# Inverse square roots on VectorE: a bit-pattern guess and three Newton steps instead of Sqrt and reciprocal, in a two-layer convolution kernel

## The chip, the cores and the metric

The kernel runs on one core of a Trainium2 chip. The metric is device time in microseconds (us) of that core, from launch to the last write. The core has five engines with their own instruction queues: TensorE (PE, matrix products into PSUM), VectorE (DVE), ScalarE (ACT), GpSimd (POOL) and SyncE (SP, which issues most DMAs). Each engine works its queue in order; an instruction waits for semaphores that other engines or DMAs set.

## The reference

The input x has shape (8, 256, 64, 64) in fp32. Two layers follow, each a residual: `x = x + L0(gn(x))` and then `x = x + L1(gn(x))`. The normalisation is a group norm over 32 groups of 8 channels, without weights:

```python
g = v.reshape(B_, G, C_ // G, H_, W_)
m = jnp.mean(g, axis=(2, 3, 4), keepdims=True)
s = jnp.var(g, axis=(2, 3, 4), keepdims=True)
return ((g - m) / jnp.sqrt(s + eps)).reshape(v.shape)
```

Layer 0 makes 3x3 kernels from the data: two 1x1 maps to 32 channels, one of them unfolded 3x3, then batch norm (with given mean and variance, so another `1 / sqrt(v + eps)`), relu, a 1x1 map, batch norm, relu, and a 1x1 map to 9 weights for each of 32 groups at each pixel. These weigh the 3x3 neighbourhood of a third 1x1 map of 256 channels.

Layer 1 is the sum of two branches, each times a rate: 7x7 local attention with 4 heads of 64 channels and reflecting edges, and two depthwise 3x3 convolutions summed with a softmax over 9 weights (a 256 to 2304 map, `Wfc`).

Inverse roots are needed for 8 images x 2 layers of group norm, and once each for the two batch norms.

## The kernel before, in words

**Tiling.** An image is cut into 8 bands of 8 rows (512 pixels); 256 channels are two tiles of 128 partitions. The main loop runs over g, the bands of all images in sequence (64 bands of layer 1). For each g there are 8 steps s (channel tile ct = s // 4, group of pixel tiles m = s % 4). Layer 0 runs 12 bands ahead of layer 1 (`AHEAD`), so g starts at -12: the first 12 bands are layer 0 alone, the following 52 do layer 1 of one band and layer 0 of a later band side by side, and the last 12 are layer 1 alone.

**Order.** Inside the main loop the order of instructions on every engine is written out by hand (`tc.manual_schedule()`). Each step has six places; `advance()` moves to the next place and emits what is due there, and `after(n, f)` puts f off by n places. Each step emits on TensorE, among others: the attention scores (`scores`, L736, even m), the weighted values (`weighted_values`, L785), transposes of the probabilities (`transposed`, L773, copied by ScalarE at L775), and two rounds of `branch_weights` (four matmuls pf at L872, then Exp on ScalarE at L877). Beside them lie parts of layer 0: `value_maps` (L369), `values` (pv, L594, copied by ScalarE at L601), `tap_weights` (pw at L464, whose two products are `prod` on VectorE at L477 and are added by GpSimd at L485), and `hidden_maps` (L418, L428, L440). VectorE further has the masked scores and their extremes (`masked`, L750), the reciprocal of the exponentials' sums (`probabilities`, L765, before ScalarE's scaling at L767), the depthwise taps (L829, L855), the output adds (L804) and the reciprocal at L893.

**Buffers.** pf, pv, pw, the projections pq and pk, the transposes ptp, the value maps p, and the small results of the normalisation (pg, pb, pgc) share one PSUM tag, "gen", with 4 buffers: the matmul that takes the fifth waits until the first has been read. The products `prod` have 2 buffers.

**The normalisation.** `gn_affine` gets the statistics of a norm and emits a chain over places: at +3 a matmul averages the means over the group (a1, L237); at +5 VectorE takes them and forms the differences (a2, L246 to L250); at +10 a second matmul (a3); at +12 VectorE adds eps (a4, L258); at +14 ScalarE takes the Sqrt in place (a5, L262); at +18 VectorE takes the reciprocal and the bias (a6, L266 and L269), and `done(sc, bi)` runs in the same place.

For layer 0 (`scaled_weights`, tiles named a, called at s = 2 of every eighth band), `done` is `scale`: ScalarE multiplies w12 and w3 by sc (L296, L297, four instructions); five places later 16 matmuls bring the bias through the weights (`through`, L304), and two places after that VectorE adds the biases (`biases`, L312 to L314). w12s and w3s have one buffer; the bands that read the old ones have been issued in the steps before. In terms of the main loop this is band 3 of an image's eight (for the next but one image, from image 2 on); image 0's norm comes before the loop and image 1's in the first 12 bands.

For layer 1 (`norm_rows`, tiles named b, called in band 6 of each image for the next one), `done` is `keep`: VectorE copies sc and bi side by side (L535, L536); three places later two products spread them over channels (`by_channel`, pgc, L542), and two places after that VectorE takes them (L547). ScalarE applies them in `normalise` (L566) from the second step of band 7 on.

The batch norms use `rstd_` (L143) at the start, before the hand-written order begins.

**Activation tables.** ScalarE's activations come from a table that has to be in place. The profile shows its loads as ACT_TABLE_LOAD, under the line of the activation that they precede. The kernel uses Sqrt, Exp, Relu, Identity and Copy.

Of the kernel before, what the change touches and what calls it, by code (L numbers as in the profile page):

```python
# [9 lines left out]

F32 = mybir.dt.float32
BF16 = mybir.dt.bfloat16
AF = mybir.ActivationFunctionType
ALU = mybir.AluOpType
AX = mybir.AxisListType
# [3 lines left out]
P = 128  # L19
# [7 lines left out]
GN_EPS = 1e-5  # L27
BN_EPS = 1e-5
# [27 lines left out]
CHUNK = R * KW  # L56
NPROB = 2 * CHUNK
NEG = -1.0e30


AHEAD = NB + 4
# [25 lines left out]
def conv_layers_kernel(ctx: ExitStack, tc: tile.TileContext, ins: dict, out: bass.AP):  # L87
    nc = tc.nc
# [3 lines left out]
    const = ctx.enter_context(tc.tile_pool(name="const", bufs=1))  # L92
# [14 lines left out]
    def load(name, shape, src=None, now=True):  # L107
        t = const.tile(shape, F32, name=f"c_{name}")
        late.append(lambda: nc.scalar.dma_start(out=t, in_=ins[name] if src is None else src))
        if now:  # L110
            late.pop()()
        return t

    gmat = load("gmat", [P, P])
    par = load("par", [P, NPAR])
# [24 lines left out]
    for t in probs + x3n + h2n:  # L140
        nc.gpsimd.memset(t, 0.0)

    def rstd_(out_, var, eps):  # L143
        nc.vector.tensor_scalar(out_, var, eps, None, ALU.add)
        nc.scalar.activation(out_, out_, AF.Sqrt)
        nc.vector.reciprocal(out_, out_)


    bn1s = const.tile([P, 3], F32, name="bn1s")
    bn1b = const.tile([P, 3], F32, name="bn1b")  # L150
    bn2s = const.tile([P, 1], F32, name="bn2s")
    bn2b = const.tile([P, 1], F32, name="bn2b")
    for s, t, g, b_, m, v, n, p in (
        (bn1s, bn1b, PG, PB, PM, PV, 3, P),
        (bn2s, bn2b, PG2, PB2, PM2, PV2, 1, P),
    ):
        rstd_(s, par[:p, v : v + n], BN_EPS)
        nc.vector.tensor_mul(s, s, par[:p, g : g + n])
        nc.vector.tensor_mul(t, s, par[:p, m : m + n])
        nc.vector.tensor_sub(t, par[:p, b_ : b_ + n], t)  # L160
# [19 lines left out]
    stat = ctx.enter_context(tc.tile_pool(name="stat", bufs=2))  # L180
# [34 lines left out]
    def after(n, f):  # L215
        later.append((place[0] + n, f))
# [8 lines left out]
    def gn_affine(sts, means, name, done):  # L225


        n = len(sts)
        mv = stat.tile([P, n, 2], F32, name=f"mv_{name}", tag=f"mv{n}")
        for ct, st in enumerate(sts):  # L230
            nc.vector.bn_aggr(mv[:, ct, :], st)
        mean, var = mv[:, :, 0], mv[:, :, 1]
        gm, d, sc, bi = (stat.tile([P, n], F32, name=f"{v}_{name}", tag=f"{v}{n}") for v in ("gm", "d", "sc", "bi"))

        def group_means(v, k):
            pg = ps.tile([P, n], F32, name=f"pg_{name}_{k}", tag="gen", bufs=4)
            nc.tensor.matmul(pg, means, v, start=True, stop=True)  # L237
            return pg


        def a1():
            pg = group_means(mean, 0)
            after(2, lambda: a2(pg))

        def a2(pg):
            nc.vector.tensor_copy(gm, pg)  # L246
            for ct in range(n):
                c = slice(ct, ct + 1)
                nc.vector.tensor_scalar(d[:, c], pg[:, c], mean[:, c], None, ALU.subtract)
                nc.vector.tensor_scalar(d[:, c], d[:, c], d[:, c], var[:, c], ALU.mult, ALU.add)  # L250
            after(5, a3)

        def a3():
            pg = group_means(d, 1)
            after(2, lambda: a4(pg))

        def a4(pg):
            nc.vector.tensor_scalar(sc, pg, GN_EPS, None, ALU.add)  # L258
            after(2, a5)

        def a5():
            nc.scalar.activation(sc, sc, AF.Sqrt)  # L262
            after(4, a6)

        def a6():
            nc.vector.reciprocal(sc, sc)  # L266
            for ct in range(n):
                c = slice(ct, ct + 1)
                nc.vector.tensor_scalar(bi[:, c], gm[:, c], sc[:, c], -1.0, ALU.mult, ALU.mult)  # L269
            done(sc, bi)  # L270

        after(3, a1)
# [15 lines left out]
    def scaled_weights(b):  # L288
# [21 lines left out]
        def biases(pb):  # L310
            im.bias = w0.tile([P, 1 + NCT], F32, tag="bias", name=f"bias_{b}")
            nc.vector.tensor_add(im.bias[:, 0:1], pb[:, 0:1], par[:, PB21 : PB21 + 1])  # L312
            for ct in range(NCT):
                nc.vector.tensor_add(  # L314
                    im.bias[:, 1 + ct : 2 + ct], pb[:, 1 + ct : 2 + ct], chan[:, ct, CB3 : CB3 + 1]
                )

        gn_affine([im.st0[:, ct] for ct in range(NCT)], gmat, f"a{b}", scale)

    def small_maps(b, i, home):  # L320
# [208 lines left out]
    def norm_rows(b):  # L529
        im = images[b]  # L530


        def keep(sc, bi):
            both = stat.tile([P, 2], F32, name=f"both_{b}", tag="both")
            nc.vector.tensor_copy(both[:, 0:1], sc)  # L535
            nc.vector.tensor_copy(both[:, 1:2], bi)  # L536
            after(3, lambda: by_channel(both))

        def by_channel(both):
            pg = ps.tile([P, NCT, 2], F32, tag="gen", name=f"pgc_{b}", bufs=4)  # L540
            for ct in range(NCT):
                nc.tensor.matmul(pg[:, ct], gc[:, ct], both, start=True, stop=True)  # L542
            after(2, lambda: take(pg))

        def take(pg):
            im.aff = stat.tile([P, NCT, 2], F32, name=f"aff_{b}", tag="aff")
            nc.vector.tensor_copy(im.aff, pg)  # L547

        gn_affine([im.st1], gq, f"b{b}", keep)
# [460 lines left out]
    with tc.manual_schedule():  # L1010

        for i, use in enumerate(("xc", "xc", "xr", "xr", "xs", None, None, None)):
            t = None
            if use is None:
                t = w1.tile([P, NCT, RP, W], F32, tag="yp", name=f"x_{i}", bufs=3)
                t = t.rearrange("p t r c -> p t (r c)")[:, :, :BAND]
# [15 lines left out]
        for g in range(-AHEAD, B * NB):  # L1032
            b, i = divmod(g, NB)
# [75 lines left out]
def _layout(inputs):  # L1109
# [59 lines left out]
    inside = (dr >= 0) & (dr < KA) & (dc >= 0) & (dc < KA)  # L1169
    arr["mask"] = np.tile(np.where(inside, 0.0, NEG).astype(f), (2, 1))  # L1170
    return {n: np.ascontiguousarray(v) for n, v in arr.items()}
# [19 lines left out]
```

## Time and profile before

| | |
|---|---|
| median of 3 runs | 3910.43 us (3908.52 to 3914.09) |
| the profiled execution | 3911.49 us, of which the trace's span is 3909.7 us |
| mean granted TensorE clock | 0.994 |
| busy: PE, DVE, ACT, POOL | 97%, 87%, 73%, 81% of the span |
| table loads | 28, of 1.283 us each |
| Sqrt activations | 18: two for batch norms, eight for each layer's group norms |
| L258 (add eps), L266 (reciprocal) | 16 each, 0.15 to 0.16 us |

"Busy" is the time in which an engine had an instruction in work. A group of the profile names the line, the engine, the operation, the tiles (result <- operands) and the count; then the busy time in us, the mean of one in ns, and the idle time just before it with what ended it. In the timeline the first column is the start from the beginning of the span, the second the length in us; "x2" merges neighbours of one line.

### The profile page before, as it was taken

How to read it: one execution, taken by the hardware profiler on the slowest of the kernel's cores; microseconds unless marked ns; L12 is line 12 of the kernel's file. 1: busy time of each engine (PE TensorE's matmuls, PEld its weight loads, DVE VectorE, ACT ScalarE, POOL GpSimd, SP SyncE). 2: the span in 40 equal slices, each digit the busy share in tenths (PEclk: the TensorE clock that was granted, in tenths of full speed). 3: DMA queues.
4: the chain of work that ended last, by engine and by line, in shares of the span. 5: the costliest groups of instructions: out<-in, count | busy, mean ns of one | idle time of the engine just before them, and what ended most of it. 6: DMA issues, size and time to landing. Idle time of an engine off the chain costs nothing.

```text
span 3909.7 us, 71679 instructions
## 1 busy us (share of the span) xinstructions
PE 3778.1 (97%) x24620; PEld 2112.2 (54%) x24620; DVE 3419.7 (87%) x7143; ACT 2835.8 (73%) x6779; POOL 3172.5 (81%) x2156
## 2 busy tenths in 40 slices
PE   5889999999999999999999999999999999999998
PEld 2445555555555555555555555555555555555554
DVE  6879898899898999899998998989988889978778
ACT  4457777777777777777777777777777777677776
POOL 4768888888887988888888888978988888956665
PEclk9999999999999999999999999999999999999999
DMA  8764443543444543543444443444433443322221
GB/s 245 208 168 128 127 118 115 143 121 116 124 123 123 142 118 105 140 131 114 139 111 128 136 119 113 127 138 116 130 111 100 133 122 94 87 85 79 72 60 35
DMA packets 429710, 473.36 MB, mean 121 GB/s; under 512 B 60992, under 2 KB 322208, under 8 KB 429088
## 3 DMA queue, kind: packets, MB, share of 16 engines
q1 hardware_dynamic: 412768, 453.01, 41.1%
q10 hardware_dynamic: 16576, 15.76, 1.3%
q8 instruction: 194, 3.18, 0.3%
q14 instruction: 172, 1.41, 0.1%
HBM read 329.08 MB, written 143.00 MB: 121 GB/s over the span
## 4 chain that ended last, share of the span: by engine, by line
PE 41%; DVE 24%; POOL 15%; ACT 11%; issue 6%; DMA 3%; SPq 0%; ACTq 0%; POOLq 0%; DVEq 0%
PE pf L872 19%; POOL xg L485 8%; DVE prod L477 7%; DVE acc L855 5%; DVE rec L893 5%; POOL ex L1087 4%; PE small L785 3%; PE pv L594 3%; ACT x L343 3%; PE ptp L773 3%; PE sco L736 3%; PE pk L692 2%; PE pq L670 2%; ACT ex L877 2%; DMA x<-x3n 2%
## 5 line engine op out<-in xcount | busy, mean ns | idle before, releaser
L872 PE MATMUL pf<-yp,c_wfc 128*128 128x512 f32 x4096 | 1916.6, 594 | 17.8 <-ACT ex L877 6.8
L485 POOL TENSOR_TENSOR xg<-xg,prod 128x1024 f32<-128x1024 f32 x549 | 1198.8, 2184 | 106.7 <-DVE prod L477 82.5
L872 PEld LDWEIGHTS pf<-yp,c_wfc 128*128 128x128 f32 x4096 | 738.5, 190 | 719.0 <-issue 629.2
L1087 POOL TENSOR_TENSOR ex<-ex,ex 128x1024 f32<-128x1024 f32 x384 | 908.2, 2365 | 66.4 <-ACT ex L877 62.5
L829 DVE SCALAR_TENSOR_TENSOR acc<-yp,c_chan,acc 128x504 f32<-128x504 f32 (+3 forms) x1104 | 775.4, 702 | 64.7 <-ACT acc L820 41.3
L477 DVE SCALAR_TENSOR_TENSOR prod<-pw,c_par,x3q 128x1040 f32<-128x1040 f32 x576 | 737.0, 1286 | 103.6 <-PE pw L464 57.4
L855 DVE SCALAR_TENSOR_TENSOR acc<-hid,c_chan,acc 128x504 f32<-128x504 f32 (+3 forms) x1024 | 750.6, 733 | 18.1
L877 ACT ACTIVATE ex<-pf 128x512 f32<-128x512 f32 x1024 | 602.0, 588 | 214.5 <-PE pf L872 197.5
L758 ACT ACTIVATE prob<-prob,nmax 128x196 f32<-128x196 f32 x1024 | 459.1, 451 | 224.5 <-DVE nmax L750 224.3
L767 ACT ACTIVATE prob<-prob,tot 128x196 f32<-128x196 f32 x1024 | 413.1, 452 | 249.5 <-DVE tot L765 248.3
L894 POOL TENSOR_TENSOR tot<-tot,rec 128x256 f32<-128x256 f32 x254 | 185.4, 730 | 398.0 <-DVE rec L893 391.6
L893 DVE RECIPROCAL rec<-tot 128x256 f32<-128x256 f32 x256 | 445.8, 1742 | 9.5 <-POOL tot L894 4.3
L775 ACT COPY pt<-ptp 112x512 f32<-112x512 f32 x511 | 295.0, 577 | 110.3 <-PE ptp L773 109.9
L750 DVE CUSTOM_DVE_ANT_0 prob<-sco,c_mask 128x196 f32<-128x196 f32 x1024 | 324.4, 354 | 28.1 <-PE sco L736 28.0
L773 PEld LDWEIGHTS ptp<-ident,prob 128*112 128x112 f32 x2044 | 227.2, 133 | 184.2 <-issue 157.1
L773 PE MATMUL ptp<-ident,prob 128*112 128x128 f32 x2044 | 319.0, 279 | 0.0
L785 PEld LDWEIGHTS small<-pt,vt 112*64 112x64 f32 x8144 | 258.2, 137 | 77.4 <-issue 75.7
L785 PE MATMUL small<-pt,vt 112*64 112x64 f32 x8144 | 293.7, 225 | 1.2 <-DMA vt<-vd 1.2
L369 PE MATMUL p<-xc,w3s 128*128 128x512 f32 x512 | 248.3, 608 | 15.8 <-ACT ex L877 15.8
L594 PE MATMUL pv<-c_wv,yp 128*128 128x256 f32 x1056 | 252.1, 381 | 7.4 <-ACT qb L674 6.0
L888 POOL TENSOR_SCALAR tot<-tot 128x512 f32<-128x512 f32 x127 | 243.6, 1918 | 11.1
L464 PEld LDWEIGHTS pw<-h2n,c_c 128*128 128x128 f32 x1152 | 176.2, 192 | 137.6 <-issue 122.7
(139 smaller groups left out, 4750.0 us busy)
## 6 DMA issues: line engine op xcount, KB each, us to landing
vt<-vd SPq DMA_DIRECT2D x512, 112.0 KB
x3q<-x SPq DMA_DIRECT2D x128, 264.0 KB
xc<-in_x SPq DMA_DIRECT2D x64, 512.0 KB
xg<-in_xg SPq DMA_DIRECT2D x64, 512.0 KB
yp<-x SPq DMA_DIRECT2D x128, 256.0 KB
xr<-x SPq DMA_DIRECT2D x64, 512.0 KB
out_x<-xr SPq DMA_DIRECT2D x64, 512.0 KB
xs<-in_x SPq DMA_DIRECT2D x57, 512.0 KB
```

The costliest lines, as they stand in the source:

```text
L477: nc.vector.scalar_tensor_tensor(prod[:, :, :RUN], pw[:, j, :RUN].unsqueeze(1).to_broadcast([P, SHARE, RUN]), par[:, PCB2 + k : PCB2 + k + 1],
L485: nc.gpsimd.tensor_add(im.xg[i], im.xg[i], rows(prod))
L758: nc.scalar.activation(prob[:, h, :NKEY], prob[:, h, :NKEY], AF.Exp, bias=nmax[:, h : h + 1], scale=-1.0, accum_out=tot[:, h : h + 1],)
L767: nc.scalar.activation(prob[:, h, :NKEY], prob[:, h, :NKEY], AF.Copy, scale=tot[:, h : h + 1])
L773: nc.tensor.transpose(ptp[:, h, ch], prob[:, h, ch * CHUNK : (ch + 1) * CHUNK], ident)
L785: nc.tensor.matmul(po[half[h], :, t * TQ : (t + 1) * TQ], im.vt[i + ch, m][:n, t, (2 * ct + h) * HD : (2 * ct + h + 1) * HD], pt[:n, h, ch ...
L829: nc.vector.scalar_tensor_tensor(o, yp[:, ct, ra + dr : rb + dr, ca + dc : cb + dc], chan[:, ct, CW1 + k : CW1 + k + 1], o, ALU.mult, ALU.add,
L855: nc.vector.scalar_tensor_tensor(o, hid[:, ra + dr : rb + dr, ca + dc : cb + dc], chan[:, ct, CW2 + k : CW2 + k + 1], o, ALU.mult, ALU.add,)
L872: nc.tensor.matmul(pf, wfc[:, kt, 2 * m + j, ct * P : (ct + 1) * P], images[b].yp[i][:, kt, PAD : PAD + R], start=(kt == 0), stop=(kt == N ...
L877: nc.scalar.activation(ex[:, j].rearrange("p (r c) -> p r c", r=R), pf, AF.Exp)
L893: nc.vector.reciprocal(rec, v)
L1087: after(4, lambda ex=ex, exb=exb: nc.gpsimd.tensor_add(ex, ex, exb))
```

## The change

The function `rstd_` no longer uses ScalarE. It adds eps on VectorE into a second tile v, reads the bits of v as an integer, shifts them right by one, takes them from the constant 0x5F3759DF (multiply by -1 and add), and reads the result as fp32: a guess of `1 / sqrt(v)`. Three Newton steps follow, each of three VectorE instructions (t = -0.5 y y; t = t v; y = (t + 1.5) y). That is 12 VectorE instructions, each using the result of the one before it.

In `gn_affine` the steps a5 and a6 are gone: a4 calls `rstd_` and then does in the same place what a6 did, the bias and `done`. So what follows (the scalings, the matmuls L304 and L542, the biases, the copies) comes six places, one step of s, earlier in the order. One small tile, va, is added to a norm's; the differences d are reused as t.

```diff
-BF16 = mybir.dt.bfloat16
+I32 = mybir.dt.int32
...
+ROOT = float(0x5F3759DF)
...
-    def rstd_(out_, var, eps):
-        nc.vector.tensor_scalar(out_, var, eps, None, ALU.add)
-        nc.scalar.activation(out_, out_, AF.Sqrt)
-        nc.vector.reciprocal(out_, out_)
+    def rstd_(out_, var, eps, v, t):
+
+        bits = out_.bitcast(I32)
+        nc.vector.tensor_scalar(v, var, eps, None, ALU.add)
+        nc.vector.tensor_scalar(bits, v.bitcast(I32), 1, None, ALU.logical_shift_right)
+        nc.vector.tensor_scalar(bits, bits, -1.0, ROOT, ALU.mult, ALU.add)
+        for _ in range(3):
+            nc.vector.scalar_tensor_tensor(t, out_, -0.5, out_, ALU.mult, ALU.mult)
+            nc.vector.tensor_mul(t, t, v)
+            nc.vector.scalar_tensor_tensor(out_, t, 1.5, out_, ALU.add, ALU.mult)
+
+    root = [const.tile([P, 3], F32, name=f"root_{i}") for i in range(2)]
...
-        rstd_(s, par[:p, v : v + n], BN_EPS)
+        rstd_(s, par[:p, v : v + n], BN_EPS, root[0][:p, :n], root[1][:p, :n])
...
-        gm, d, sc, bi = (stat.tile([P, n], F32, name=f"{v}_{name}", tag=f"{v}{n}") for v in ("gm", "d", "sc", "bi"))
+        gm, d, sc, bi, va = (stat.tile([P, n], F32, name=f"{v}_{name}", tag=f"{v}{n}") for v in ("gm", "d", "sc", "bi", "va"))
...
         def a4(pg):
-            nc.vector.tensor_scalar(sc, pg, GN_EPS, None, ALU.add)
-            after(2, a5)
-
-        def a5():
-            nc.scalar.activation(sc, sc, AF.Sqrt)
-            after(4, a6)
-
-        def a6():
-            nc.vector.reciprocal(sc, sc)
+            rstd_(sc, pg, GN_EPS, va, d)
             for ct in range(n):
                 c = slice(ct, ct + 1)
                 nc.vector.tensor_scalar(bi[:, c], gm[:, c], sc[:, c], -1.0, ALU.mult, ALU.mult)
             done(sc, bi)
```

## The prediction

> **What bounds the kernel now.** First the page: the busy row, the chain that ended last, the costliest group.
>
> ```profile
> PE 3778.1 (97%) x24620; PEld 2112.2 (54%) x24620; DVE 3419.7 (87%) x7143; ACT 2835.8 (73%) x6779; POOL 3172.5 (81%) x2156
> ...
> PE 41%; DVE 24%; POOL 15%; ACT 11%; issue 6%; DMA 3%; SPq 0%; ACTq 0%; POOLq 0%; DVEq 0%
> ...
> L872 PE MATMUL pf<-yp,c_wfc 128*128 128x512 f32 x4096 | 1916.6, 594 | 17.8 <-ACT ex L877 6.8
> ```
>
> TensorE is the busiest, then VectorE; ScalarE, which the change relieves, has 27% free. Four pf matmuls follow each other in some 1.72 us all through the trace, so in steady state whatever delays TensorE is lost. Second, the stretches table, cut at the first pf matmul of each of six bands of one image (band 2, 3, 5 and 6 shown; first column the stretch, then its length and the busy time of TensorE, its weight loads, VectorE, ScalarE, GpSimd).
>
> ```profile
> 831.70:889.20 57.50, 57.15 (x380) 31.96 (x380) 52.29 (x107) 43.21 (x104) 50.47 (x35) 1.00 0.44 127
> 889.20:949.60 60.40, 59.37 (x401) 33.65 (x400) 54.40 (x121) 47.13 (x111) 52.98 (x37) 1.00 0.45 127
> 1007.20:1065.00 57.80, 57.20 (x380) 32.01 (x380) 52.56 (x108) 43.10 (x106) 51.17 (x36) 1.00 0.43 121
> 1065.00:1122.80 57.80, 56.18 (x380) 31.52 (x379) 53.02 (x116) 43.45 (x106) 50.63 (x35) 1.00 0.39 107
> ```
>
> Band 3 holds the layer-0 root ("a"), band 6 the layer-1 root ("b"). Band 6, table switches and all, is as long as band 5. Band 3 is 2.9 us longer, of which 1.39 us are its own 16 bias matmuls (L304). So the switches cost far less than they last.
>
> Third, the groups of ScalarE, for what is removed.
>
> ```profile
> L262 ACT ACT_TABLE_LOAD x13 | 16.7, 1283 | 0.2
> L877 ACT ACT_TABLE_LOAD x13 | 16.7, 1283 | 0.2
> L145 ACT ACT_TABLE_LOAD x1 | 1.3, 1283 | 6.8 <-DMA c_chan<-in_chan 6.8
> L758 ACT ACT_TABLE_LOAD x1 | 1.3, 1283 | 0.0
> ```
>
> Fourth, the order of time around one "a" root, VectorE (columns: start, length, engine, line, operation).
>
> ```profile
> 910.02 0.21 DVE L249 TENSOR_SCALAR d_a<-pg_a,mv_a 128x1 f32<-128x1 f32 x1
> 910.26 0.27 DVE L250 TENSOR_SCALAR d_a<-d_a,mv_a 128x1 f32<-128x1 f32 x1
> ...
> 917.90 0.15 DVE L258 TENSOR_SCALAR sc_a<-pg_a 128x2 f32<-128x2 f32 x1
> 917.97 1.29 DVE L477 SCALAR_TENSOR_TENSOR prod<-pw,c_par,x3q 128x1040 f32<-128x1040 f32 x1
> ...
> 920.25 1.29 DVE L477 SCALAR_TENSOR_TENSOR prod<-pw,c_par,x3q 128x1040 f32<-128x1040 f32 x1
> ...
> 924.47 0.16 DVE L266 RECIPROCAL sc_a<-sc_a 128x2 f32<-128x2 f32 x1
> 924.66 0.33 DVE L269 TENSOR_SCALAR bi_a<-gm_a,sc_a 128x1 f32<-128x1 f32 x2
> ```
>
> A small instruction that needs the one before it starts 0.20 us later (L266 to L269; 0.24 us from L249 to L250); one that does not, 0.07 us later (L258 to L477). VectorE has no gap here. TensorE beside it, and a "b" root's one gap (last line):
>
> ```profile
> 916.06 0.61 PE L464 MATMUL pw<-h2n,c_c 128*128 128x132 f32 x4
> ...
> 921.40 1.89 PE L594 MATMUL pv<-c_wv,yp 128*128 128x256 f32 x8
> 923.13 1.88 PE L872 MATMUL pf<-yp,c_wfc 128*128 128x512 f32 x4
> ...
> 1104.06 1.98 PE L872 MATMUL pf<-yp,c_wfc 128*128 128x512 f32 x4 [0.76 <-ACT ex L877]
> ```
>
> **Removed: ScalarE's part.** 28 loads of 1.283 us and 18 roots of 0.20 us, 39.5 us of ScalarE. After the load at L758 no other comes until the next Sqrt, through Copy, Identity, Relu and Exp, so without Sqrt one load is left, and it sits before the start's first activation. On TensorE's path the 26 loads in steady state are worth at most the gap: 0.76 us at each of 7 "b" roots (5.3 us), about nothing at the "a" roots, where TensorE runs through. The load at L758 (238.5 us) stands in the chain, so -1.28 us; bounds 0 and -1.28. The load that is left runs either in the 6.8 us that the queue idles at the start or just before L296, where w12s is not needed until the 2.51 us of L304 are over: 0, at worst +1.28.
>
> **Added: VectorE's part.** L258 and L266 give way to 12 instructions, each needing the last: 12 x 0.20 = 2.4 us. Bounds: 12 x 0.07 = 0.84 (as if none waited) and 12 x 0.24 = 2.9; I take 0.20, since the row is of the same size, engine and dependence. Three or two more (the bi pair 0.27; for "b" bi and the two copies 0.40) move up from after the reciprocal. So the product that started at 917.97 starts at 917.90 + 2.4 + 0.27 = 920.57, 2.6 us late ("b": 2.7).
>
> Queued behind on VectorE: two products (L477), the row minima (L750, ScalarE's exponentials wait), two output adds, four taps, the reciprocal of the sums (L765, ScalarE's probabilities wait). The tag "gen" has four PSUM buffers, so the pf at 923.13 takes the buffer of the pw at 916.06, read last by the product at 920.25, which ends at 921.54. Slack: 923.13 - 921.54 = 1.59 us ("b": 1098.48 - 1096.90 = 1.58). **"a", 6 times in steady state:** 2.6 - 1.6 = +1.0 us each. ScalarE's four weight scalings move up with the root: it waits for sc at 919.5 until 920.3, then they delay the transposed copy at 919.89 to 921.6, whose buffer is asked for at 924.85: nothing. The 16 bias matmuls come one step sooner, the same 1.39 us. The old values of w12s and w3s were last read in steps 0 and 1, so no wait is added. **"b", 7 times:** pgc's matmuls come a step sooner and take that buffer, so TensorE waits 1.1 us; then L765 ends at 1101.1 instead of 1098.4, L767 and L601 follow, and the next pf starts at 1102.4 instead of 1100.64; the gap of 0.76 goes and pgc's 0.44 has been paid already, so the pf of 1104.06 starts near 1104.6: +0.5 each. The last image's has no products around it: 0. Sum 6 x 1.0 + 6 x 0.5 = +9; bounds 0.07 us a step: no wait, -5.3; 0.24 us a step: 6 x 1.5 + 7 x 1.0 = +16. GpSimd's sums of products (L485) start about 1.2 us late and regain it in its gaps. No step that moves issues a DMA; SP and GpSimd's queue are not passed by one.
>
> **Start.** Image 0: L258 at 24.31 to L269 at 24.94 was 0.63 us, becomes 2.4, with all engines waiting: +1.75 (0.2 to 2.3). Image 1: the scalings go in front of the hidden map at 146.44 on ScalarE (they had followed it): +1.3 (0 to 2.5). Image 0's "b" at 201: 0 (to +1). The two batch norms: 24 small instructions for 4 on VectorE, which idles 1.18 + 0.87 + 1.08 us before 13.31: +0.3 (0 to 1.4). With -1.28: +2.1 (-1.1 to +7).
>
> **Sum:** 9 + 2 = +11 us. The profiled execution took 3911.49 us (span 3909.7 and 1.8 around it), 1.06 above the median of the runs; on the median 3910.4 + 11 = 3921.5 us.
>
> **A rule against a row.** The row: a dependent small step every 0.20 us, 2.4 us in all. The Trainium skill's "VectorE: DVE Perf Modes" (the TRN2 errata) counts 58 cycles plus the elements at 0.96 GHz, an estimate of 0.06 us for two elements, 0.75 us for twelve: below the slack, so no loss. The same page says to minimise the number of chained operations, which speaks against this change. On the loads, "ScalarE: Activation LUTs" (What ACT_TABLE_LOAD costs) adds a drain of 1.38 us to each; here the activation starts 0.01 us after the load ends (load 922.56 + 1.28, Sqrt 923.86). With the page's drain the 26 loads would last 69 us, by the rows 33.
>
> **Rivals.** *The steps overlap.* If they follow in less than about (1.59 + 0.07 - 0.27)/12 = 0.12 us, the delay stays inside the slack and the removed gaps are all that shows: -5.3 and the start's -1 to +2, about 3906. For: L258 to L477 in 0.07. Against: L249 to L250, L266 to L269. *ScalarE decides.* If the switch pairs held up the kernel, 13 x 2.57 = 33 us go: 3877. For: ex at L877 waits behind a load 13 times. Against: band 6 is no longer than band 5. *No slack at all.* If a later wait (minima, sums, GpSimd) passes on the whole insertion, 13 x 2.7 = +35, with the start's 2: 3947. For: VectorE has no gap from 909 to 924 us. Against: TensorE's next demand is 1.6 us off. *The loads stay.* With Sqrt gone nothing needs a second table; then +16 and 3926.
>
> **How the numbers follow.** Forecast 0.58, overlap 0.20, ScalarE 0.04, no slack 0.16, loads stay 0.02. A measurement here tells 0.2%, 7.8 us. The forecast's own range, 3913 to 3933, lies over +7.8 for 0.45 and under for 0.13. Overlap: 0.17 same, 0.03 faster. So faster 0.07, same 0.30, slower 0.63. The range 3907 to 3936 takes in most of the overlap and the low half of no slack.
>
> **What would show it.** One table load; 12 small VectorE steps about 0.20 us apart; band 3 near 61.4, band 6 near 58.3 us, the others unchanged; a wait of about 1 us of pf or pgc on prod L477; the first L304 at 27 us. Steps 0.1 us apart, or a pf that still starts 1.72 us after pv, would make it wrong; so would a start that hides or doubles its 2 us.

## The result, and the profile after

| | before | after |
|---|---|---|
| median, us | 3911.4 (3908.52 to 3914.09) | 3965.73 (3964.15 to 3966.02) |
| the profiled execution, us | 3911.49 | 3965.67 (span 3963.9) |
| mean granted TensorE clock | 0.994 | 0.988 |
| table loads | 28 | 1 |

The ratio of after to before is 1.0139 [1.0123, 1.0155]: 54 us slower, where +11 was forecast and 3936 was the upper end. The page of the changed kernel: the busy row, the chain's shares by engine, and two groups.

```profile
PE 3802.5 (96%) x24620; PEld 2121.2 (54%) x24620; DVE 3477.8 (88%) x7323; ACT 2810.9 (71%) x6734; POOL 3176.4 (80%) x2156
...
PE 41%; DVE 28%; POOL 11%; ACT 10%; issue 5%; DMA 3%; SPq 0%; ACTq 0%; POOLq 0%; DVEq 0%
...
L871 PE MATMUL pf<-yp,c_wfc 128*128 128x512 f32 x4096 | 1928.9, 597 | 41.5 <-ACT ex L876 20.7
...
L295 ACT ACT_TABLE_LOAD x1 | 1.3, 1283 | 8.3 <-DMA c_w<-in_w 8.3
```

VectorE did 180 more instructions and was busy 58 us longer. That is 0.32 us for each one added, where an unhindered one here lasts 0.16. The pf matmuls' idle time went from 17.8 to 41.5 us. Their busy time also grew, by 12.3 us, although there are as many as before: some of them ran slower.

The stretches table says where. These are bands 3, 5 and 6 of the same image as before (length, then the busy time of TensorE, its weight loads, VectorE, ScalarE, GpSimd, then the granted clock).

```profile
905.30:970.00 64.70, 61.59 (x401) 34.51 (x399) 58.32 (x131) 45.23 (x108) 53.55 (x37) 0.97 0.44 121
1027.60:1085.50 57.90, 57.26 (x381) 32.04 (x380) 52.62 (x110) 43.26 (x105) 51.26 (x36) 1.00 0.43 121
1085.50:1147.10 61.60, 57.91 (x380) 32.27 (x379) 56.94 (x125) 41.09 (x103) 51.14 (x36) 0.97 0.37 101
```

Band 3 (the "a" root) is 64.7 us where it was 60.4, band 6 (the "b" root) 61.6 where it was 57.8, and band 5, with no root, is as long as before. Over all images, each "a" root costs 2.8 us (four times) or 4.3 (twice), each "b" root 3.7 to 4.3, the last "b" 0.8. Bands without a root stay within 0.1 us, save the first of all (0.9). That makes some 45 us. The start, up to the first pf, took 244.9 us where it took 236.9: the other 8.

VectorE's timeline of that "a" root (start, length) shows what the roots lost.

```profile
934.02 0.15 DVE L147 TENSOR_SCALAR va_a<-pg_a 128x2 f32<-128x2 f32 x1
934.21 0.36 DVE L148 TENSOR_SCALAR sc_a<-va_a 128x2 int32<-128x2 int32 x1
934.60 2.29 DVE L149 TENSOR_SCALAR sc_a<-sc_a 128x2 int32<-128x2 int32 x1
936.92 0.16 DVE L151 SCALAR_TENSOR_TENSOR d_a<-sc_a 128x2 f32<-128x2 f32 x1
937.12 0.16 DVE L152 TENSOR_TENSOR d_a<-d_a,va_a 128x2 f32<-128x2 f32 x1
...
938.94 1.29 DVE L476 SCALAR_TENSOR_TENSOR prod<-pw,c_par,x3q 128x1040 f32<-128x1040 f32 x1
```

GpSimd at the same time:

```profile
930.09 4.45 POOL L484 TENSOR_TENSOR xg<-xg,prod 128x1024 f32<-128x1024 f32 x2
934.50 2.36 POOL L1086 TENSOR_TENSOR ex<-ex,ex 128x1024 f32<-128x1024 f32 x1
```

Two elements per partition took 2.29 us. L148 ends at 934.57, as L484 does (934.54). L149 then ends at 936.89, as L1086 does (936.86). The steps after it, with GpSimd idle until 940.38, take 0.16 us and follow each other at 0.20, as forecast. The group of L149 over the whole run (shortest, median and longest in ns) shows this is the rule, and that image 0's root at 24.2 us does not suffer:

```profile
L149 DVE TENSOR_SCALAR sc_a<-sc_a x8: 170/2280/2286, 24.2 to 2847.3; 128x2 int32<-128x2 int32 x8
L149 DVE TENSOR_SCALAR sc_b<-sc_b x8: 153/154/156, 207.8 to 3484.5; 128x1 int32<-128x1 int32 x8
```

With one column (b) L149 is never held. There the first step with two SBUF operands is, and the one behind it. VectorE's timeline of the "b" root:

```profile
1114.18 0.15 DVE L149 TENSOR_SCALAR sc_b<-sc_b 128x1 int32<-128x1 int32 x1
1114.37 0.41 DVE L151 SCALAR_TENSOR_TENSOR d_b<-sc_b 128x1 f32<-128x1 f32 x1
1114.81 2.28 DVE L152 TENSOR_TENSOR d_b<-d_b,va_b 128x1 f32<-128x1 f32 x1
1117.12 0.16 DVE L153 SCALAR_TENSOR_TENSOR sc_b<-d_b,sc_b 128x1 f32<-128x1 f32 x1
```

and GpSimd's:

```profile
1110.31 4.45 POOL L484 TENSOR_TENSOR xg<-xg,prod 128x1024 f32<-128x1024 f32 x2
1114.71 2.36 POOL L1086 TENSOR_TENSOR ex<-ex,ex 128x1024 f32<-128x1024 f32 x1
```

From eps to the product behind the root it is 4.92 us at "a" (934.02 to 938.94) and 5.01 at "b" (1113.81 to 1118.82), where before it was 0.07. VectorE is 4.9 us late, not 2.6. TensorE's timeline then shows gaps (in brackets: idle time and what ended it), one of 1.19 us at "a" and one of 3.06 at "b":

```profile
940.60 1.98 PE L871 MATMUL pf<-yp,c_wfc 128*128 128x512 f32 x4 [1.19 <-ACT pt L774]
...
1119.04 0.57 PE L541 MATMUL pgc<-both,c_gc 128*128 128x2 f32 x4
1122.67 2.71 PE L871 MATMUL pf<-yp,c_wfc 128*128 128x512 f32 x4 [3.06 <-ACT ex L876]
```

The way from VectorE to these gaps leads through ScalarE, whose instructions read the buffers that the pf matmuls take. ScalarE at "a", then at "b":

```profile
938.69 0.35 ACT L295 ACTIVATE w12s<-c_w,sc_a 128x64 f32<-128x64 f32 x1 [3.07 <-DVE sc_a L153]
...
939.98 0.56 ACT L774 COPY pt<-ptp 112x512 f32<-112x512 f32 x1
...
1120.43 0.46 ACT L757 ACTIVATE prob<-prob,nmax 128x196 f32<-128x196 f32 x1 [4.05 <-DVE nmax L749]
...
1122.04 0.58 ACT L876 ACTIVATE ex<-pf 128x512 f32<-128x512 f32 x1
```

At "a" the copy of the transposes stands behind the four scalings of the weights, which wait 3.07 us for the root; it ends at 940.54, and the pf starts at 940.60. At "b" ScalarE waits 4.05 us for VectorE's row minima; the ex behind them ends at 1122.62, and the pf starts at 1122.67.

The four pf matmuls after the second gap take 2.71 us instead of some 1.9. Three stretches of 3.4 us around that gap tell why; the 1.00 or 0.50 is the granted clock:

```profile
1120.40:1123.80 3.40, 1.13 (x3) 0.66 (x4) 3.37 (x8) 2.33 (x7) 3.30 (x2) 1.00 0.68 111
1123.80:1127.20 3.40, 3.40 (x8) 1.85 (x8) 2.49 (x6) 1.88 (x4) 3.32 (x3) 0.50 0.17 40
1127.20:1130.60 3.40, 3.40 (x12) 1.67 (x12) 3.37 (x8) 1.95 (x6) 3.23 (x3) 1.00 0.20 49
```

For 3.4 us after the gap the clock is halved. This happens at 642, 1124, 1602, 2080, 2557 and 3035 us, all six "b" roots that have such a gap, and at 946 and 2858 us, two "a" roots, which are the two that cost 4.3 us. The other four "a" roots have the same gaps without it; what tells them apart is not shown.

So the first reading, for the experiments to test: a VectorE instruction that reads two SBUF tensors, or moves two columns from SBUF to SBUF by tensor_scalar, waits until the GpSimd instruction in work has ended, however small it is. The Trainium skill's "SBUF — State Buffer" (Who interferes with whom) has a rule for two SBUF operands: the second comes through ports that VectorE shares with GpSimd, and whoever has them keeps them for a whole instruction. The 2.28 and 2.29 us beside 0.16 agree with it.

### The profile page after: what moved, and what is told of

Its sections match the earlier page's. It is cut to its first block, busy times and chain, and to the rows that moved or that the text cites. A ratio compares the mean times of both kernels' runs of the same rounds, so it can differ in the third digit from the quotient of the medians.

```text
span 3963.9 us, 71813 instructions
## 1 busy us (share of the span) xinstructions
PE 3802.5 (96%) x24620; PEld 2121.2 (54%) x24620; DVE 3477.8 (88%) x7323; ACT 2810.9 (71%) x6734; POOL 3176.4 (80%) x2156
## 4 chain that ended last, share of the span: by engine, by line
PE 41%; DVE 28%; POOL 11%; ACT 10%; issue 5%; DMA 3%; SPq 0%; ACTq 0%; POOLq 0%; DVEq 0%
PE pf L871 20%; DVE prod L476 8%; DVE acc L854 6%; POOL xg L484 6%; DVE rec L892 5%; PE small L784 3%; PE pv L593 3%; PE ptp L772 3%; POOL ex L1086 3%; PE sco L735 3%; ACT x L342 3%; PE pk L691 3%; PE pq L669 3%; DMA x<-x3n 2%; DVE acc L828 2%
## 5 line engine op out<-in xcount | busy, mean ns | idle before, releaser
L871 PE MATMUL pf<-yp,c_wfc 128*128 128x512 f32 x4096 | 1928.9, 597 | 41.5 <-ACT ex L876 20.7
L484 POOL TENSOR_TENSOR xg<-xg,prod 128x1024 f32<-128x1024 f32 x549 | 1201.0, 2188 | 149.8 <-DVE prod L476 117.5
L1086 POOL TENSOR_TENSOR ex<-ex,ex 128x1024 f32<-128x1024 f32 x384 | 908.3, 2365 | 64.4 <-ACT ex L876 60.7
L749 DVE CUSTOM_DVE_ANT_0 prob<-sco,c_mask 128x196 f32<-128x196 f32 x1024 | 324.7, 355 | 24.2 <-PE sco L735 24.2
```

What stands on the lines that cost most here:

```text
L484: nc.gpsimd.tensor_add(im.xg[i], im.xg[i], rows(prod))
L871: nc.tensor.matmul(pf, wfc[:, kt, 2 * m + j, ct * P : (ct + 1) * P], images[b].yp[i][:, kt, PAD : PAD + R], start=(kt == 0), stop=(kt == N ...
L1086: after(4, lambda ex=ex, exb=exb: nc.gpsimd.tensor_add(ex, ex, exb))
```

## The experiments

Theory A of the expectations is this wait. Theory C is the earlier place in the order, and B what lies in the chain itself wherever its operands are. All are single edits, of the kernel after or of the kernel before, as the text says. "Per root" is the length of band 3 ("a") or band 6 ("b") against the kernel before.

**One SBUF operand per step (psum).** The kernel after, with the two scratch values in PSUM beside pg; same place in the order, as many steps.

```diff
+    def rstd_psum(out_, var, eps, v, t):
+        v32, t32 = v.bitcast(I32), t.bitcast(I32)
+        nc.vector.tensor_scalar(v, var, eps, None, ALU.add)
+        nc.vector.tensor_scalar(t32, v32, 1, None, ALU.logical_shift_right)
+        nc.vector.tensor_scalar(out_.bitcast(I32), t32, -1.0, ROOT, ALU.mult, ALU.add)
+        for _ in range(3):
+            nc.vector.scalar_tensor_tensor(t, out_, -0.5, v, ALU.mult, ALU.mult)
+            nc.vector.tensor_mul(t, t, out_)
+            nc.vector.scalar_tensor_tensor(out_, t, 1.5, out_, ALU.add, ALU.mult)
...
-            pg = ps.tile([P, n], F32, name=f"pg_{name}_{k}", tag="gen", bufs=4)
+            pg = ps.tile([P, 3 * n], F32, name=f"pg_{name}_{k}", tag="gen", bufs=4)
...
-            rstd_(sc, pg, GN_EPS, va, d)
+            rstd_psum(sc, pg[:, :n], GN_EPS, pg[:, n : 2 * n], pg[:, 2 * n :])
```

> The changed kernel with v and t of the group norms' root in PSUM (columns beside pg), so that each of the 12 steps reads one tensor from SBUF at most; same number of steps, same order. Theory A (a step that reads two SBUF tensors, or is an SBUF to SBUF tensor_scalar of even length, waits for the GpSimd instruction in work): no step lasts over 0.3 us, the chain is near 2.4 us, TensorE's gaps at the roots are about 1 us and mostly do not slow its clock; 3915 to 3932 us. Theory B (the burst of twelve dependent steps in itself, wherever its operands lie): the gaps stay at 3 us, 3955 to 3975 us.

Measured: 3925.28 us (3923.24 to 3926.99), ratio 1.0039 [1.0024, 1.0054]. The same root on VectorE, and GpSimd beside it:

```profile
924.51 0.17 DVE L159 TENSOR_SCALAR pg_a<-pg_a 128x2 int32<-128x2 int32 x1
924.72 0.16 DVE L160 TENSOR_SCALAR sc_a<-pg_a 128x2 int32<-128x2 int32 x1
924.91 0.17 DVE L162 SCALAR_TENSOR_TENSOR pg_a<-sc_a,pg_a 128x2 f32<-128x2 f32 x1
```

```profile
920.39 4.43 POOL L495 TENSOR_TENSOR xg<-xg,prod 128x1024 f32<-128x1024 f32 x2
924.78 2.36 POOL L1097 TENSOR_TENSOR ex<-ex,ex 128x1024 f32<-128x1024 f32 x1
```

GpSimd is as busy as before over these steps, and none waits. Bands 3 and 6:

```profile
895.60:956.40 60.80, 59.67 (x401) 33.72 (x400) 55.71 (x131) 44.89 (x108) 52.10 (x37) 1.00 0.44 122
...
1071.80:1130.50 58.70, 56.44 (x380) 31.60 (x379) 54.72 (x127) 40.82 (x103) 50.63 (x35) 1.00 0.37 105
```

An "a" root now costs 0.4 us, a "b" root 0.9, and past 264 us no stretch at half clock is left. Moving two small tiles takes back 40 of the 54 us. The access wait, with what follows from it, is shown as the main cause; the chain's length alone is not.

**The old place for bias and `done` (late).** The kernel after, with one `after(6, a6)` between root and bias.

```diff
             rstd_(sc, pg, GN_EPS, va, d)
+            after(6, a6)
+
+        def a6():
```

> The changed kernel, but bias and what follows come six places after the root, as before the change. Theory A: VectorE still stands still behind GpSimd for the same 2.3 us, so most of the loss stays: 3945 to 3965 us; at an a root ScalarE no longer waits 3 us before L295, which may take 1 us off each. Theory C (the earlier order of the scalings and small matmuls makes the loss): 3910 to 3925 us.

Measured: 3963.61 us (3961.3 to 3968.48), ratio 1.0139 [1.0124, 1.0154], as slow as after. An "a" root costs 3.3 us, not less than the 2.8 of after, and a "b" root 3.4 to 6.2. That the scalings, pgc and the copies come a step sooner is not the cause. At "a" the delay only takes another way to TensorE: its gaps there, 1.28 and 0.93 us, now end with ScalarE's ex.

**The wait alone, without the change (two_sbuf, one_sbuf).** The kernel before gets two small products on VectorE after the eps step: once with both operands in SBUF, once with one of them in PSUM. Nothing uses the results.

```diff
+            nc.vector.tensor_mul(d[:, :1], gm[:, :1], mean[:, :1])
+            nc.vector.tensor_mul(d[:, :1], d[:, :1], mean[:, :1])
```

```diff
+            nc.vector.tensor_mul(d[:, :1], pg[:, :1], mean[:, :1])
+            nc.vector.tensor_mul(d[:, :1], pg[:, :1], d[:, :1])
```

> The kernel before with two more VectorE instructions right after L258, 128x1 each and the second needing the first, each reading two SBUF tensors; their result is not used. Theory A: one of the two lasts 2 us or more at each steady root (the GpSimd instruction L1087 starts within 0.5 us of L258), VectorE is 2.5 to 3 us late, 1 to 1.5 us past TensorE's slack of 1.6 us; 3920 to 3950 us. Theory B: two steps are 0.4 us, inside the slack; 3905 to 3916 us, same as one_sbuf.

> The control of two_sbuf: the same two instructions, but each reads one tensor from SBUF and one from PSUM. Both theories: 0.4 us, inside TensorE's slack; 3908 to 3916 us, no instruction over 0.3 us.

Measured: 3947.53 us (3941.21 to 3951.54), ratio 1.0100 [1.0083, 1.0116], against 3911.35 us (3907.92 to 3916.82), ratio 1.0004 [0.9995, 1.0014]. VectorE, and then GpSimd, with both operands in SBUF:

```profile
915.04 0.48 DVE L259 TENSOR_TENSOR d_a<-gm_a,mv_a 128x1 f32<-128x1 f32 x1
915.55 2.29 DVE L260 TENSOR_TENSOR d_a<-d_a,mv_a 128x1 f32<-128x1 f32 x1
...
911.05 4.45 POOL L487 TENSOR_TENSOR xg<-xg,prod 128x1024 f32<-128x1024 f32 x2
915.45 2.37 POOL L1089 TENSOR_TENSOR ex<-ex,ex 128x1024 f32<-128x1024 f32 x1
```

VectorE with one operand in PSUM, while GpSimd's additions ran from 913.32 to 917.77:

```profile
917.30 0.15 DVE L259 TENSOR_TENSOR d_a<-pg_a,mv_a 128x1 f32<-128x1 f32 x1
917.48 0.16 DVE L260 TENSOR_TENSOR d_a<-pg_a,d_a 128x1 f32<-128x1 f32 x1
```

Two instructions on 128 numbers cost 36 us over the run when both operands lie in SBUF and nothing measurable otherwise. An "a" root cost 1.9 us. A "b" root cost 2.2 us where no half-clock stretch followed, 3.8 with one of 3.4 us, 5.0 with two: each such stretch goes with 1.1 to 1.6 us more.

**What the removed half was worth (noload).** The kernel before with Copy in place of Sqrt: the square root is left out, so the loads go, while places and chain stay.

```diff
-        nc.scalar.activation(out_, out_, AF.Sqrt)
+        nc.scalar.activation(out_, out_, AF.Copy)
...
-            nc.scalar.activation(sc, sc, AF.Sqrt)
+            nc.scalar.activation(sc, sc, AF.Copy)
```

> The kernel before with Copy in place of Sqrt at both places, so that no second activation table is needed: it leaves the square root out (it multiplies by the reciprocal of the variance), everything else stays. It prices the table loads alone. My prediction's terms: 5.3 us at the b roots, nothing at the a roots, 1.3 us at the start: 3901 to 3907 us. If ScalarE were the limit, 33 us would go: 3875 to 3885 us. If the loads are hidden altogether: 3909 to 3913 us.

Measured: 3908.05 us (3902.75 to 3911.96), ratio 0.9995 [0.9986, 1.0003]. TensorE's gap at the "b" root, ScalarE before it, and band 6:

```profile
1095.47 1.98 PE L872 MATMUL pf<-yp,c_wfc 128*128 128x512 f32 x4 [0.74 <-ACT ex L877]
```

```profile
1093.95 0.46 ACT L758 ACTIVATE prob<-prob,nmax 128x196 f32<-128x196 f32 x1 [1.52 <-DVE nmax L750]
...
1094.85 0.57 ACT L877 ACTIVATE ex<-pf 128x512 f32<-128x512 f32 x1
```

```profile
1056.40:1114.30 57.90, 56.24 (x381) 31.59 (x380) 53.08 (x117) 41.04 (x104) 50.71 (x35) 1.00 0.38 106
```

The gap of 0.76 us that the forecast credited to the table loads is 0.74 without them. It ends with ScalarE's ex, at 1095.42, and ScalarE had waited 1.52 us for VectorE's row minima before it: without the loads it is VectorE that makes the gap. Bands 3 and 6 are as long as before within 0.04 us in all images, so the 26 loads in steady state, 33 us of ScalarE, cost nothing. What the change could win by all its loads is the 2 us that this run shows, by its interval 5.5 at most.

**The root as a scalar operand (ptr), and spread over places (spread).** The kernel after with the value of the row before as tensor_scalar's per-partition scalar, so that each step reads one SBUF tensor, column by column; in spread, each Newton step moreover in a place of its own, and bias and `done` six places later.

```diff
-            rstd_(sc, pg, GN_EPS, va, d)
+            guess(pg)
+            for k in range(3):
+                newton()
...
+        def newton():
+            for ct in range(n):
+                c = slice(ct, ct + 1)
+                nc.vector.tensor_scalar(va[:, c], d[:, c], sc[:, c], sc[:, c], ALU.mult, ALU.mult)
+            for ct in range(n):
+                c = slice(ct, ct + 1)
+                nc.vector.tensor_scalar(sc[:, c], va[:, c], 1.5, sc[:, c], ALU.add, ALU.mult)
```

In spread, against ptr:

```diff
-            for k in range(3):
-                newton()
+            for k in range(3):
+                after(1 * (k + 1), newton)
+            after(6, a6)
+
+        def a6():
```

> The changed kernel with other instructions for the group norms' root: eps added from PSUM twice (v and -v/2), the integer steps column by column, and each Newton step as two tensor_scalar instructions of one column whose y comes as a scalar operand per partition, so that no instruction reads two SBUF tensors; 18 instructions for an a root, 10 for a b root, all in one place. Theory A: no step over 0.35 us, an a root some 2.6 us long, a b root 2.2; 3915 to 3930 us, like psum. Theory B (burst, not access): 3950 us and over.

> ptr, but with the guess in the place of a4, one Newton step in each of the three places after it, and the bias and what follows six places after the guess, as before the change. Theory A: VectorE is never more than 1 us late at once, inside TensorE's slack of 1.6 us, so the roots cost nothing and the loads' gaps are gone; with the start's 2 to 4 us 3904 to 3912 us, the first version that is not slower than before. If the slack is no real slack, each root costs about its 2.6 us all the same: 3930 us and over.

Measured: 3924.28 us (3923.02 to 3928.07), ratio 1.0038 [1.0024, 1.0052] for ptr; 3927.53 us (3924.59 to 3932.41), ratio 1.0046 [1.0033, 1.0060] for spread. In ptr no step lasts over 0.28 us, an "a" root costs 0.5 and a "b" root 0.8. A second way around the shared operand gives what the first gave. Spreading gains nothing: an "a" root costs 1.0, a "b" root 0.5 to 0.6 twice and 2.1 to 2.3 the four times that a half-clock stretch follows. In the image shown above TensorE has gaps of 0.71 us at "a" and 1.68 at "b", both ended by ScalarE's ex; why the later places are no better is not shown.

**A shorter chain (ptr2).** As ptr with two Newton steps, so with a less exact root.

```diff
-            for k in range(3):
+            for k in range(2):
                 newton()
```

> ptr with two Newton steps instead of three (the result is less exact): VectorE is delayed by 2.0 us at a root instead of 2.6. By the buffer that pf or pgc takes from pw, TensorE has 1.6 us of slack there, so an a root's loss falls from 0.5 to about 0, a b root's from 0.8 to 0.2; 3914 to 3920 us, the rest being the start. If each 0.6 us of VectorE counts in full: 13 x 0.6 = 8 us less as well, so the bands decide, not the total.

Measured: 3920.0 us (3915.94 to 3923.64), ratio 1.0022 [1.0013, 1.0032]; "a" 0.4, "b" 0.25. The four steps that go at "a" and two at "b" are worth 4 us in all, nearly all of it at "b". At "a", where 0.5 us should have fallen to about 0, 0.4 is left.

**Newton on GpSimd (gps).** The kernel after with eps and the integer steps on VectorE and four GpSimd instructions per Newton step; bias and `done` six places later.

```diff
...
+            for _ in range(3):
+                nc.gpsimd.tensor_mul(d, sc, sc)
+                nc.gpsimd.tensor_mul(d, d, va)
+                nc.gpsimd.tensor_scalar(d, d, -0.5, 1.5, ALU.mult, ALU.add)
+                nc.gpsimd.tensor_mul(sc, sc, d)
+            after(6, a6)
```

> The changed kernel with VectorE doing eps and the integer guess (column by column) and GpSimd the Newton steps (four instructions each), bias and what follows six places after the guess. No VectorE instruction needs two SBUF tensors. If GpSimd's twelve small steps (about 0.2 us each, 2.4 us) fit in its free fifth: 3905 to 3915 us. If GpSimd's sums come late and hold up VectorE's products through their two buffers: 3920 to 3945 us.

Measured: 3960.03 us (3955.93 to 3966.04), ratio 1.0128 [1.0111, 1.0145], above both of the expectations. An "a" root costs 2.3 us, a "b" root 4.2 to 5.5, with the clock halved for 3.4 or 6.8 us behind each of six "b" roots. Its 12 instructions follow at 0.27 us, so 3.2 us are put into GpSimd's queue, ahead of the sums that the products wait for:

```profile
1116.28 1.30 DVE L491 SCALAR_TENSOR_TENSOR prod<-pw,c_par,x3q 128x1040 f32<-128x1040 f32 x1 [1.28 <-POOL xg L499]
```

**Does the gap halve the clock? (filler)** The kernel after, with 12 matmuls right after pgc at the "b" roots of images 1 to 7, into unused columns of its buffer. They do no work; they fill TensorE's gap.

```diff
+            pg = ps.tile([P, 2 * NCT + P], F32, tag="gen", name=f"pgc_{b}", bufs=4)
...
+            for _ in range(12 if b else 0):
+                nc.tensor.matmul(pg[:, 2 * NCT :], ident, gmat, start=True, stop=True)
```

> The changed kernel with 12 more matmuls (ident by gmat, 128 columns, some 2.7 us of TensorE, into spare columns of pgc's buffer, never read) right after pgc at the b roots of images 1 to 7, where TensorE stands 3.06 us before the next pf. Theory D (the gap itself halves the granted clock for the next 3.4 us): the slow stretches at the b roots go, band 6 falls from +3.8 to about +2.2 us against before; 3952 to 3960 us. If the clock falls for another reason, or the gap is no idle time that matmuls can fill: no fall, 3964 us and over.

Measured: 3961.89 us (3961.61 to 3962.64), ratio 1.013 [1.0115, 1.0145]. TensorE at the same root, and the granted clock over 10.2 us from VectorE's first product there:

```profile
1114.95 2.92 PE L543 MATMUL pgc<-c_gmat,ident 128*128 128x128 f32 x24
1118.14 1.98 PE L873 MATMUL pf<-yp,c_wfc 128*128 128x512 f32 x4 [0.27 <-ACT ex L878]
```

```profile
1112.80:1123.00 10.20, 9.74 (x53) 7.01 (x52) 9.92 (x29) 4.63 (x14) 7.08 (x4) 1.00 0.68 124
```

All six half-clock stretches at "b" roots are gone, only two at "a" roots are left (1897 and 2853 us), and a "b" root costs 3.2 to 3.3 us instead of 3.7 to 4.3. So the gap does halve the clock, shown, but that is worth only 0.5 to 1.0 us of a "b" root here. The last image, which had no gap to fill, pays 3.4 us for the idle work where it paid 0.8.

**The start (steady, s_a0, s_a1, s_b0, bnonly).** In steady, the kernel after does the roots of images 0 and 1 (a0, a1) and of image 0's second layer (b0) in the old way; in the next three only one of them is new (`name in ("a1", "b0")` for s_a0, and so on). In bnonly, the kernel before gets the new root for the two batch norms alone.

```diff
+            if name in ("a0", "a1", "b0"):
+                nc.vector.tensor_scalar(sc, pg, GN_EPS, None, ALU.add)
+                after(2, a5)
+            else:
+                rstd_(sc, pg, GN_EPS, va, d)
+                a7()
...
```

> The changed kernel, but the group norms of layer 0's images 0 and 1 and of layer 1's image 0, all before the first band of layer 1, keep Sqrt, reciprocal and their old order. Against the changed kernel it prices the start. My prediction's term: +2 us (with the batch norms +0.3 in it), so 3963 us. By the totals less the bands' sums the start's share is 6 to 9 us: 3955 to 3960 us.

> steady with layer 0's root of image 0 in the new form too (24 us into the run, where GpSimd is idle and every engine waits for it). By the rows of the chain +1.2 to +1.8 us against steady, 3958 to 3959 us. If the whole 9 us start here, through transfers that come later: 3963 us and over.

> steady with layer 0's root of image 1 in the new form too (147 us into the run, beside GpSimd's sums). Prediction's term +1.3 us; with one step that waits 2.0 us for GpSimd +2 to +4 us against steady: 3959 to 3961 us. If this root makes the start's share: 3963 us and over.

> steady with layer 1's root of image 0 in the new form too (some 205 us into the run). Prediction's term 0; with one step that waits for GpSimd 0 to +3 us against steady: 3957 to 3960 us. If this root makes the start's share: 3963 us and over.

> The kernel before with the two batch norms' roots by the new steps and the group norms' by Sqrt as before: the start's share of the batch norms. My prediction's term: +0.3 us (0 to 1.4), 3909 to 3913 us. If the 24 small instructions hold up the first statistics: 3914 us and over.

Measured:

| kernel | median, us | ratio |
|---|---|---|
| steady | 3956.89 (3952.88 to 3957.41) | 1.0115 [1.0100, 1.0130] |
| s_a0 | 3956.88 (3953.19 to 3958.53) | 1.0113 [1.0096, 1.0130] |
| s_a1 | 3955.99 (3955.03 to 3956.89) | 1.0114 [1.0099, 1.0129] |
| s_b0 | 3955.4 (3952.81 to 3955.79) | 1.0111 [1.0096, 1.0126] |
| bnonly | 3910.35 (3907.69 to 3912.88) | 1.0000 [0.9991, 1.0009] |

The three roots of the start cost 8.8 us together (3965.73 - 3956.89). Against the kernel before as it ran beside each, steady is 45.7 us slower and the kernels with one new root 48.2 (a0), 47.3 (a1) and 46.7 (b0), so one root alone comes to 1.1 to 2.6 us; but each of these has an interval of some 6 us either way, so they tell neither the parts nor whether the parts add up to the 8.8. The batch norms cost nothing that can be told. How the 8.8 us divide stays open; the time to the first pf varies between single profiles of kernels that differ little there, from 229.0 to 245.7 us, so one pair of profiles settles nothing. The clock may have a part: up to the first pf its mean is 0.90 in after, 0.93 in before and in steady. No run separates it.

## Why the prediction was wrong

**The step that failed is "12 x 0.20 = 2.4 us".** The spacing of 0.20 us is right wherever a step is not held. But its row, L249 to L250 and L266 to L269, is of instructions that read one SBUF tensor at most. The working took them as "of the same size, engine and dependence" and did not look at where the operands lie. The new steps read SBUF twice, beside a GpSimd that is busy 81% of the span. In the trace of before, VectorE's large steady instructions with two tensors each have one in PSUM (the product reads pw, the adds read the attention's sums), and no row there that the working used shows the wait. A row that it did not use does. L200, in the start, subtracts one SBUF tensor from another, twice:

```profile
56.57 4.20 DVE L200 TENSOR_TENSOR c_wfc<-c_wfc,last 128x2048 f32<-128x2048 f32 x1
...
72.53 2.28 DVE L200 TENSOR_TENSOR c_wfc<-c_wfc,last 128x2048 f32<-128x2048 f32 x1
```

The first stands beside a GpSimd instruction that ends at 58.62, 2.15 us before it; the second runs with GpSimd idle. The bounds of the working, 0.07 and 0.24 us a step, both left it out. Measured: 4.9 us from eps to the product, of which 2.3 to 2.4 are the wait. Runs psum, ptr and two_sbuf against one_sbuf show it from three sides, and it is worth 40 of the 54 us with the clock's part in it.

**A second step was wrong, and the number does not show it: "the pf at 923.13 takes the buffer of the pw at 916.06, read last by the product".** In psum VectorE is as late as the forecast had it (the product starts 2.63 us after eps). The second product and the pf of that place:

```profile
929.24 1.29 DVE L487 SCALAR_TENSOR_TENSOR prod<-pw,c_par,x3q 128x1040 f32<-128x1040 f32 x1
```

```profile
929.55 1.88 PE L882 MATMUL pf<-yp,c_wfc 128*128 128x512 f32 x4
```

The pf starts 0.98 us before the product ends, straight behind pv, so it does not wait for it, although it is the fifth that takes a buffer. At "b" pgc starts at 1105.30 while the product runs from 1105.06 to 1106.35. So the slack of 1.59 us was taken to an instruction that neither waits for. What does end TensorE's gaps at the roots is ScalarE: in after the copy of the transposes, for which the working put "nothing", and the ex behind the row minima.

**The rest of the sum can be held against psum, where the wait is absent.** The forecast of +11 us meets +15 there (3925.28 against 3910.42 in that comparison), inside the range. Term by term:

- "a", +1.0 each: measured 0.4, and not by the wait forecast. TensorE is idle for 1.13 us of band 3 in psum and for 1.03 in before, and busy 0.3 us longer; ptr2, with a shorter chain, has 0.4 too. What the 0.4 is stays open, and that it lies near 1.0 supports nothing.
- "b", +0.5 each: measured 0.9. The credit for the loads, 0.76 us each, was wrong: noload has the gap without them. In psum that gap is gone from its place all the same, and TensorE has two new ones a little earlier, 0.81 and 0.19 us, both ended by ScalarE. The forecast had 1.1 us there, as a wait of pgc for the product.
- The last "b", 0: 0.0 in psum, 0.8 in after.
- Start, +2.1: 8.8 by steady. The part for the batch norms, +0.3, is 0.0. The +1.75 and +1.3 of images 0 and 1 lie below what a run with one of them alone can tell. This term is the one whose cause is not settled.

**The table loads.** One is left, as said, and it ran at 8.3 us with nothing waiting for it. "About nothing at the 'a' roots" holds; the whole removal is worth at most the 2 us of noload.

**The rivals.** *The steps overlap* falls: 0.20 us between free steps. *ScalarE decides* falls with noload. *The loads stay* falls: one load. *No slack at all* named 3947 and is nearest in size, but not in kind. It passed the whole insertion of 2.7 us on; here the insertion was 4.9 us, and 2.8 at "a" and 3.8 at "b" came through. That is less than its length, so some slack there was, if not the one that was forecast.

**What would have shown it.** Three of the signs came as announced: one table load, free steps 0.20 us apart, the first bias matmul at 26.45 us (27 was forecast). Bands 3 and 6 did not: 64.7 and 61.6 us, where 61.4 and 58.3 were named. In psum they are 60.8 and 58.7. Nor did the wait of pf or pgc for the product: ScalarE ends the gaps. The start was to hide its 2 us or double them if the forecast was wrong; it took 8.

## What to carry to other kernels

Before a chain of small instructions is put on VectorE, ask of each where its operands lie and what GpSimd does meanwhile: two SBUF tensors beside a GpSimd instruction of 2.2 us make a step of 0.16 us last up to 2.3 us, and an operand in PSUM or passed as a per-partition scalar avoids it. A price from a row holds only if the row shares the operands' places, and not only size, engine and dependence. And before crediting the removal of table loads, find what ends the wait they stand beside: here 26 of them were worth nothing, so there was nothing to pay for the added chain. A slack that is worked out from an order of buffers is a guess until a run in which the reader comes late shows that the taker waits for it.

## What the runs showed of the hardware

- **An access wait of VectorE on GpSimd**, 2.27 to 2.30 us for a 128x1 product with both operands in SBUF at the steady roots but the last (two_sbuf), 0.16 us with one in PSUM (one_sbuf), beside GpSimd's additions too. A tensor_scalar from SBUF to SBUF is held with two columns (2.29 us) and not with one (0.15 us).
- **The clock falls after a short gap.** TensorE's granted clock went to 0.50 for 3.4 us after idle gaps of 3.06 us, six times of six, and after the shorter gaps (1.19 us the longest) of two "a" roots of six. The Trainium skill's "TensorE: Matmul & The Clock Gate" (HAM oscillation — how this bites in real kernels) names idle gaps of over some 3.4 us as the danger; here shorter ones sufficed, and the measurement decides. Filling the gaps of 3.06 us kept the clock at 1.00.
- **Dependent small instructions on GpSimd** follow at 0.27 us (gps), VectorE's at 0.20.
- **A table load may run long before its activation**: at 8.3 us, while the activation it precedes came at 26.2 us.
